# Loading one block's rows in two halves, the first in a tile of its own, in a fused graph-attention kernel

## The chip, the cores and the metric

The kernel runs on one core of a Trainium2 chip. The metric is the device time of one execution in microseconds (us); a kernel's time is the median of several runs. Times inside an execution come from one profiled execution and count from the start of its span.

## What is computed

The input x has 128 batches of 64 rows of 768 numbers, with a 64 by 64 adjacency for each batch. The rows are normalised, then two graph-attention layers follow, and x is added at the end:

```python
h = jnp.maximum(_layernorm(x, axis=-1), 0.0)
for l in range(2):
    m_left  = jnp.einsum('bsh,oh->bso', h, W_left[l])
    m_right = jnp.einsum('bsh,oh->bso', h, W_right[l])
    u_left  = jnp.einsum('bih,bjh->bij', h, m_left) / temper
    u_right = jnp.einsum('bih,bjh->bij', h, m_right) / temper
    u = u_left * adj_tri + u_left * diag_mask + u_right * jnp.swapaxes(adj_tri, 1, 2)
    delta_exp_u = jnp.exp(u) * adj
    attention = delta_exp_u / (jnp.sum(delta_exp_u, axis=2, keepdims=True) + 1e-10)
    h_lin = jnp.einsum('bsh,oh->bso', h, W_lin[l]) + b_lin[l]
    ctx = jnp.matmul(attention, h_lin)
    h = jax.nn.relu(_layer_norm(ctx, ln_a[l], ln_b[l]))
return x + h
```

## The kernel before

**Blocks.** The 128 batches are cut into 16 blocks of 8 batches (512 tokens). A block is needed with features on the partitions (tile ht), while x has tokens on them. Each layer is two passes: pass_one makes the projections for the scores, the scores and the softmax; pass_two makes the linear part, the context and the row norm. The change touches pass_one of the first layer (l = 0).

**Products.** pass_one takes two blocks at a time (U = 0 to 7). For each U, project (L511) runs 29 products (PRODUCTS), a scheme that saves multiplications by forming sums of weight blocks and of token blocks first. Each product is done for the left weight and then for the right one, eight matmuls each (L523). The results lie in PSUM banks (X, Y, Z for left; V and right for right), and read (L293) copies or adds them into the tile m: the first use of a part by ScalarE (ACT, L303), every later one by an add on VectorE (DVE, L221). A bank is used again only when it has been read.

**Slots.** The order of all other work is written out by hand. put(slot, f) puts work at a numbered slot; project calls run four times per product, after half of the matmuls of each side and after its read, so slot 4i is in product i and a U has 116 slots (SLOTS). Within a slot, work is issued in the order in which it was put. Each engine then works through its own queue in order. All DMAs of this stage are issued by SyncE (SP), in program order too.

**The first U.** first (L558) has no ready weights. It loads the raw weights, makes the weight sums product by product on DVE and GpSimd (POOL) (weight_ops), in free 128x512 places, and after each product stores the two weights used to DRAM (keep_weight, L194), from where later U stream them (stream, L197; five of them are issued after product 25). It also prepares blocks 0 and 1 straight from x, in eight row groups n: stats, inverse, norm, turn (transposes on TensorE, L633) and settle. Groups 4 to 7 have slots of their own (L673).

**Blocks 2 to 15 of layer one.** Each goes through DRAM. load_rows (L360) loads a block's rows with eight DMAs into two halves of the buffer ROOM, always the same place; each half holds two of the four row tiles xr[q]. transpose_rows (L384) then gives a list: four statistics (mean_var, DVE, L338 and L339), four empty slots, scale (L394 on ACT, L395 and L396 on DVE), four norms (ACT, L399), two empty slots, four transposes on DVE (L415) into another part of ROOM, and a store of four DMAs (L411) into KEPT. load_h (L371) reads the block back as ht. In U = 0 the third block (u = 2) is loaded at slot 3 and its list begins at slot 26, so its last transposes are at 41 to 44 and its store at 51. The fourth (u = 3) is loaded at 52, right after; its statistics are at 62 to 65, scale at 70, norms at 71 to 74, transposes at 77 to 80, the store at 87, the read back at 103 and the load of the fifth block at 112. These lines set it:

```python
727                        slot = max(slot + 15, (92, 103)[n]) if U == 0 and l == 0 else slot + 15
735                        starts = (8, 52) if U else (26, 62)
```

Of the kernel before, what the change touches and what calls it, by code (L numbers as in the profile page):

```python
# [10 lines left out]
F32 = mybir.dt.float32  # L11
# [6 lines left out]
def kernel(  # L18
# [12 lines left out]
    nc = tc.nc  # L31
    B, S, H = x.shape
    L = w_lin.shape[0]
    P = 128
# [5 lines left out]
    Q = 4  # L40
# [24 lines left out]
    def put(slot, *fs):  # L65
        plan.setdefault(slot, []).extend(fs)
# [73 lines left out]
    def room(n, m):  # L140
        return ROOM[:, n * K2 * D:(n + m) * K2 * D]
# [140 lines left out]
    SLOTS = 4 * NP  # L282
# [29 lines left out]
    KEPT = [[dram.tile([P, C, T], F32, name=f"h{l}_{u}") for u in range(NB)] for l in range(L)]  # L312
# [22 lines left out]
    def mean_var(mv, halves):  # L335
        st = stat.tile([P, 2, 6], F32, name="st", bufs=2)
        for n in range(2):
            nc.vector.bn_stats(st[:, n, :], halves[n])  # L338
        nc.vector.bn_aggr(mv, st)  # L339


    XR = {}
# [3 lines left out]
    def new_ht():  # L346
        turns.rotate(-1)
        return big.tile([P, C, T], F32, name=f"ht{turns[-1]}", bufs=1)

    def rows_tile(pool, g):  # L350
        if pool is not None:
            return pool.tile([P, 2, H], F32, name="x", bufs=2)
        return room(3 * g, 3).rearrange("p (a h) -> p a h", a=2)

    def blocks_tile(pool):
        if pool is not None:
            return pool.tile([P, H // 32, Q, 32], F32, name="xb", bufs=1)
        return room(6, 6).rearrange("p (b q j) -> p b q j", q=Q, j=32)

    def load_rows(l, u, pool=None):  # L360

        XR[l, u] = []
        for g in range(2):
            t = rows_tile(pool, g)
            for a in range(4):
                i = 4 * g + a
                src = x[u * NBB + i] if l == 0 else ROWS[u][i]
                nc.sync.dma_start(t[a * 32:(a + 1) * 32], src.rearrange("(k j) h -> j k h", k=2))
            XR[l, u].extend([t[:, 0, :], t[:, 1, :]])

    def load_h(which, l, u):  # L371
        ht = HT[which, l, u] = new_ht()
        nc.sync.dma_start(ht, KEPT[l][u])
# [10 lines left out]
    def transpose_rows(l, u, pool=None):  # L384

        xr, todo = XR[l, u], []
        if l == 0:
            mv = stat.tile([P, Q, 2], F32, name="mv0", bufs=2)
            sd = stat.tile([P, Q], F32, name="sd0", bufs=2)
            rs = stat.tile([P, Q], F32, name="rs0", bufs=2)  # L390
            nb = stat.tile([P, Q], F32, name="nb0", bufs=2)

            def scale():
                nc.scalar.activation(sd, mv[:, :, 1], AF.Sqrt, bias=eps_in)  # L394
                nc.vector.reciprocal(rs, sd)  # L395
                nc.vector.scalar_tensor_tensor(nb, mv[:, :, 0], -1.0, rs, op0=ALU.mult, op1=ALU.mult)  # L396

            def norm(q):
                nc.scalar.activation(xr[q], xr[q], AF.Relu, bias=nb[:, q:q + 1], scale=rs[:, q:q + 1])  # L399

            norms = [lambda q=q: norm(q) for q in range(Q)]
            stats = [lambda q=q: mean_var(mv[:, q, :], [xr[q][:, :HH], xr[q][:, HH:]]) for q in range(Q)]
            for f in stats + none * (4 * (u < 4)) + [scale] + norms:
                todo.extend([f] + none * (u >= 4))
            todo.extend(none * (2 * (u < 4)))
        xb = blocks_tile(pool)

        def store():
            to = KEPT[l][u].rearrange("(b i) c t -> i c b t", b=4)
            for a in range(4):  # L410
                nc.sync.dma_start(to[:, :, :, a * P:(a + 1) * P],  # L411
                                  xb[a * 32:(a + 1) * 32].rearrange("i (c b) q j -> i c b (q j)", b=4))

        for q in range(Q):
            todo.append(lambda q=q: nc.vector.transpose(  # L415
                xb[:, :, q, :], xr[q].rearrange("p (b j) -> p b j", j=32)))
            todo.extend(none * (l or u >= 4))
        todo.append(store)
        return todo

# [6 lines left out]
    def pass_one(l, aside):  # L427
        with (tc.tile_pool(name=f"ps_one{l}", bufs=1, space=bass.MemoryType.PSUM) as ps,
# [129 lines left out]
            def first():  # L558
# [40 lines left out]
                p = ps_st.tile([P, 2 * TH], F32, name="V")  # L599
# [10 lines left out]
                def stats(n):  # L610
                    mean_var(mv[:, n, :], [xs[n][:, :HH], xs[n][:, HH:]])
                    nc.scalar.activation(sd[:, n:n + 1], mv[:, n, 1:], AF.Sqrt, bias=eps_in)
# [32 lines left out]
                def weight_ops(i, kind):  # L645
                    eng = nc.gpsimd if kind == "r" and i > 1 and i not in (12, 13) else nc.vector
                    return [lambda op=op: weight_op(ss, kind, op, eng) for op in W_OPS if op[0] == i]
# [22 lines left out]
                for i in range(2, NP):  # L670
                    fs = weight_ops(i, "l") + weight_ops(i, "r")
                    put_all(max(2, 4 * (i - 1) - 3), fs)
                for n, (s0, s1, s2, s3) in {4: (3, 4, 5, 8), 5: (6, 7, 8, 12), 6: (13, 14, 15, 19),  # L673
                                            7: (17, 18, 20, 24)}.items():
                    put(s0, lambda n=n: stats(n))
                    put(s1, lambda n=n: inverse(n))
                    put(s2, lambda n=n: norm(n))
                    put(s3, lambda n=n: turn(n), lambda n=n: settle(n))
                put(3, lambda: load_rows(0, 2))
                count = {}  # L680
                for op in X_OPS:
                    n = count[op[0]] = count.get(op[0], 0) + 1
# [28 lines left out]
            for U in range(NU):  # L711
                if U:
                    weights, done = streamed(U)
                if l or U:
                    put_token_ops(l, U, "after")
                if l == 0 and U == 1:
                    for n in range(2):
                        put(20 + 6 * n, lambda n=n: nc.sync.dma_start(KEPT[0][n], HT[1, 0, n]))
                if U + 1 < NU:
                    def block(n, slot):  # L720
                        u = 2 * U + 2 + n
                        *todo, store = transpose_rows(l, u)
                        slot = put_all(slot, todo)
                        put(slot + 6, store)
                        if u + 1 < NB:
                            put(SLOTS - 4 if U == 0 and l == 0 and n else slot + 7, lambda: load_rows(l, u + 1))
                        slot = max(slot + 15, (92, 103)[n]) if U == 0 and l == 0 else slot + 15
                        put(slot, lambda: load_h(1, l, u))
                        if l:
                            put_all(slot + 20, affine(1, l, u))  # L730

                    if l:
                        starts = (6 if U else 20, 48)
                    else:
                        starts = (8, 52) if U else (26, 62)
                    for n, slot in enumerate(starts):
                        put(slot - 1, lambda n=n, slot=slot: block(n, slot))
                    if U:
                        for n in range(2):
                            steps = softmax(2 * U - 2 + n)  # L740
                            slot = put_all(20 + 40 * n if l else (34, 76)[n], steps[:6], 2)
                            slot = put_all(slot, steps[6:] + [lambda n=n: load_adj(2 * U + n)])
                            put(slot + 11, masked(2 * U + n))
                    else:
                        for n in range(2):
                            put((40 if l else 106) + 2 * n, masked(n))
                    put_token_ops(l, U + 1, "before")
                else:
                    for n in range(2):
                        put(12 + 28 * n, lambda n=n: load_h(2, l, n))  # L750
                        put_all(38 + 28 * n, affine(2, l, n))
                    for n in range(2):
                        steps = softmax(2 * U - 2 + n)
                        put_all(put_all(14 + 28 * n, steps[:6], 2), steps[6:])
                    put(40, lambda: load_adj(2 * U))
                    put(54, masked(2 * U))
                    put(SLOTS - 24, lambda: load_adj(2 * U + 1))
                    put(SLOTS - 10, masked(2 * U + 1))
                    put_sums_t((2, l, 0), 94, 2, 85)
                if U in aside:  # L760
                    aside[U]()
                project(U, weights, done)
                assert not plan, sorted(plan)
# [420 lines left out]
```

## Time and profile before

| what | us |
|---|---|
| median of 3 runs | 2721.56 |
| lowest and highest run | 2718.0, 2725.38 |
| the profiled execution | 2719.48 |
| its span | 2717.7 |
| DVE transposes of rows into ROOM in the first 145 us (L415), median of one | 0.97 |
| DMA from 37.39 to 60.34 us, GB/s | 172 |
| DMA from 97.33 to 129.58 us, GB/s | 279 |

In the timelines below, a line is a run of like instructions: its start, its duration, the engine, the line of the code, the operation, the tile written and the tiles read, the shape, the count, and in brackets the idle time ahead of it with what ended that. PE is TensorE. In the slices, a digit is the busy share in tenths of one fortieth of the span (68 us). U = 0 lasts until about 128 us, so it lies in the first two slices. An engine's idle time costs something only if the engine that sets the end waits for it.

### The profile page before, as it was taken

Reading aid. Unit: us, or ns where it says so; the run is one execution under the profiler, and the core shown is the slowest. Engines: PE = TensorE matmul, PEld = TensorE weight load, DVE = VectorE, ACT = ScalarE, POOL = GpSimd, SP = SyncE. Lnnn points to the kernel's source line nnn. Section 1 sums busy time; section 2 is a strip of 40 time slices with the busy share of each in tenths; the row PEclk is TensorE's granted clock in tenths of the full one; section 3 lists DMA queues with packets and bytes.
Section 4 is the critical chain, followed back from the end, with each engine's and each line's share of the span. In section 5 each row is a group of like instructions: output and inputs, shape, how many; then the busy total and the mean of one; then the engine's idle time right before and its main releaser. Section 6 shows DMA issues by size and latency. Waiting matters only on the chain.

```text
span 2717.7 us, 47304 instructions
## 1 busy us (share of the span) xinstructions
PE 2681.2 (99%) x18514; PEld 2302.4 (85%) x18514; DVE 1503.8 (55%) x2458; ACT 829.7 (31%) x1615; POOL 1381.4 (51%) x1071
## 2 busy tenths in 40 slices
PE   8899999999999999999999999999999999999998
PEld 7788888888888888888788888888888888888886
DVE  7655755646556433334334645545446475666667
ACT  4031231321310154454631221221212214444443
POOL 5624244333345766566343235334243286887886
PEclk9999999999999999999999999999999999999999
DMA  7886867869666345557585966858659524655655
GB/s 246 264 288 220 277 203 235 264 202 287 213 204 213 98 136 160 195 155 244 185 280 173 308 201 227 267 194 292 214 195 306 196 97 128 182 159 160 183 158 148
DMA packets 310222, 567.81 MB, mean 209 GB/s; under 512 B 62832, under 2 KB 190064, under 8 KB 301808
## 3 DMA queue, kind: packets, MB, share of 16 engines
q1 hardware_dynamic: 309840, 564.39, 65.0%
q8 instruction: 148, 2.42, 0.4%
q14 instruction: 74, 0.61, 0.1%
q10 hardware_dynamic: 160, 0.39, 0.0%
HBM read 429.40 MB, written 135.27 MB: 208 GB/s over the span
## 4 chain that ended last, share of the span: by engine, by line
PE 93%; DVE 2%; DMA 1%; SPq 1%; issue 0%; ACT 0%; DVEq 0%
PE right L523 17%; PE X L1044 12%; PE X L523 11%; PE V L523 10%; PE Z L523 9%; PE Y L523 9%; PE V L1044 8%; PE Y L1044 6%; PE both L465 5%; PE Z L1044 4%; PE aux L852 2%; PE aux L875 1%; PE Y L875 0%; DMA wp<-ws 0%; DVE m L221 0%
## 5 line engine op out<-in xcount | busy, mean ns | idle before, releaser
L221 POOL TENSOR_TENSOR ts<-ht 128x512 f32<-128x512 f32 x352 | 480.1, 1370 | 158.4 <-PE X L1044 65.8
L221 POOL TENSOR_TENSOR ts<-ht,ts 128x512 f32<-128x512 f32 x192 | 252.8, 1323 | 348.9 <-PE V L523 208.4
L523 PE MATMUL right<-ts,wp 128*128 128x252 f32 (+1 forms) x1632 | 380.9, 376 | 1.5 <-DVE wp L221 1.5
L523 PEld LDWEIGHTS right<-ts,wp 128*128 128x128 f32 x1632 | 310.0, 190 | 40.4 <-DVE wp L221 1.9
L474 POOL TENSOR_TENSOR wm<-adj,tri 128x256 f32<-128x256 f32 x60 | 42.3, 728 | 497.7 <-DMA adj<-in_adj_dram 263.7
L221 DVE TENSOR_TENSOR m<-m,X 128x512 f32<-128x512 f32 x160 | 105.5, 684 | 262.1 <-ACT m L303 183.7
L221 DVE TENSOR_TENSOR m<-m,right 128x504 f32<-128x504 f32 (+1 forms) x304 | 199.4, 673 | 86.3 <-PE right L523 72.4
L1044 PE MATMUL X<-room,ts 128*128 128x256 f32 x1024 | 244.0, 380 | 0.1
L523 PE MATMUL Z<-ts,wp 128*128 128x256 f32 x992 | 234.6, 379 | 0.1
L221 POOL TENSOR_TENSOR ts<-ht,ht 128x512 f32<-128x512 f32 x128 | 163.7, 1289 | 139.3 <-PE right L523 93.6
L1044 PEld LDWEIGHTS X<-room,ts 128*128 128x128 f32 x1024 | 191.7, 190 | 31.7 <-issue 1.8
L523 PEld LDWEIGHTS Z<-ts,wp 128*128 128x128 f32 x992 | 188.3, 190 | 25.2 <-issue 0.4
L523 PE MATMUL X<-ts,wp 128*128 128x256 f32 x872 | 207.5, 381 | 0.0
L523 PE MATMUL V<-ts,wp 128*128 128x252 f32 (+1 forms) x864 | 201.6, 376 | 0.0
L303 ACT ACTIVATE m<-right 128x504 f32<-128x504 f32 (+1 forms) x64 | 36.1, 590 | 509.3 <-PE both L465 489.3
L523 PEld LDWEIGHTS X<-ts,wp 128*128 128x128 f32 x872 | 164.4, 190 | 23.6 <-issue 0.4
L380 ACT ACTIVATE ht<-ht,b_col,a_col 128x512 f32<-128x512 f32 x192 | 140.8, 803 | 142.0 <-DMA ht<-h 142.0
L1044 PE MATMUL Y<-room,ts 128*128 128x256 f32 x768 | 182.5, 379 | 0.0
L523 PEld LDWEIGHTS V<-ts,wp 128*128 128x128 f32 x864 | 164.2, 190 | 20.4
L1044 PEld LDWEIGHTS Y<-room,ts 128*128 128x128 f32 x768 | 145.8, 190 | 20.4 <-issue 0.6
L221 DVE TENSOR_TENSOR m<-m,Y 128x512 f32<-128x512 f32 x144 | 95.8, 683 | 118.4 <-PE Y L523 102.6
L1010 POOL TENSOR_TENSOR z<-z,b 128x768 f32<-128x768 f32 x62 | 112.7, 1831 | 89.7 <-DVE z L1007 89.7
(222 smaller groups left out, 4850.1 us busy)
## 6 DMA issues: line engine op xcount, KB each, us to landing
wp<-ws SPq DMA_DIRECT2D x435, 512.0 KB, 6.2
ht<-h SPq DMA_DIRECT2D x62, 1536.0 KB, 8.7
h<-room SPq DMA_DIRECT2D x112, 384.0 KB, 7.1
z<-z SPq DMA_DIRECT2D x128, 192.0 KB, 3.1
ws<-wp SPq DMA_DIRECT2D x93, 256.0 KB, 4.2
xr<-in_x_dram SPq DMA_DIRECT2D x120, 192.0 KB, 3.7
out_dram<-xr SPq DMA_DIRECT2D x120, 192.0 KB, 2.6
room<-in_x_dram SPq DMA_DIRECT2D x112, 192.0 KB, 5.3
```

Of the source, the lines that this page charges most:

```text
L221: (eng.tensor_add if sign == "+" else eng.tensor_sub)(o, a, b)
L303: nc.scalar.activation(to(o), p, AF.Copy, scale=1.0 if sign == "+" else -1.0)
L380: nc.scalar.activation(ht, ht, AF.Relu, bias=cols[1][:, c:c + 1], scale=cols[0][:, c:c + 1])
L465: nc.tensor.matmul(p[h * S + e:h * S + e + 32, q, e:e + 95], ht[:, c, b * S + e:b * S + e + 32], mb[:, e:e + 95], start=(c == 0), stop=(c ...
L474: nc.gpsimd.tensor_tensor(wm[:, :, k], adj[:, :, 1 - k], tri[:, k].unsqueeze(1).to_broadcast([P, Q, S]), op=ALU.mult)
L523: nc.tensor.matmul(p[:, g], wk[:, c, g * P:(g + 1) * P], tk[:, c, :].rearrange("p (b s) -> p b s", s=S)[:, :, :ns], start=(new and g == c ...
L852: nc.tensor.matmul(cx[k][i, m, :HH], at[j, q, :], hl[j, q, m * HH:(m + 1) * HH], start=True, stop=True)
L875: nc.tensor.matmul(parts[r, k][n][i], at[j, q, :], hl[j, q, cut], start=True, stop=True)
L1010: nc.gpsimd.tensor_add(zs[k], zs[k], rows["b"])
L1044: nc.tensor.matmul(p[:, n], b[t][:, c, r * P:(r + 1) * P], w[s][:, c, :], start=(i in FIRST and i not in PRELOAD and n == c == 0), stop=(c ...
```

## The change

The fourth block's rows (u = 3 of layer one) are loaded in two halves. The first half (four DMAs) gets a tile of its own, "own", of 128 x 2 x 768 numbers, and is loaded at slot 12; the second half is loaded into ROOM at slot 52, where all eight loads were. Statistics of the first half are at slots 57 and 60 and of the second at 66 and 68, scale at 72, norms at 74 to 77, transposes at 79, 81, 82 and 83. The store stays at 87 and the load of the fifth block at 112; the read back goes from 103 to 101. Row group 7 of the first two blocks moves from slots 17, 18, 20, 24 to 15, 16, 18, 23. The transposes and the store move into a function, turned, that transpose_rows calls; for other blocks the order stays what it was.

```diff
-    def load_rows(l, u, pool=None):
+    def load_rows(l, u, pool=None, halves=(0, 1), own=None):
 
-        XR[l, u] = []
-        for g in range(2):
-            t = rows_tile(pool, g)
+        XR.setdefault((l, u), [])
+        for g in halves:
+            t = rows_tile(pool, g) if own is None else own
             for a in range(4):
...
+        def turned(xr, pool):
+            xb = blocks_tile(pool)
+
+            def store():
+                to = KEPT[l][u].rearrange("(b i) c t -> i c b t", b=4)
+                for a in range(4):
+                    nc.sync.dma_start(to[:, :, :, a * P:(a + 1) * P],
+                                      xb[a * 32:(a + 1) * 32].rearrange("i (c b) q j -> i c b (q j)", b=4))
+
+            return [lambda q=q: nc.vector.transpose(
+                xb[:, :, q, :], xr[q].rearrange("p (b j) -> p b j", j=32)) for q in range(Q)], store
...
+            if u == 3:
+                return stats, scale, norms, turned(xr, pool)
...
-                                            7: (17, 18, 20, 24)}.items():
+                                            7: (15, 16, 18, 23)}.items():
...
                 put(3, lambda: load_rows(0, 2))
+                own = sp.tile([P, 2, H], F32, name="own", bufs=1)
+                put(12, lambda: load_rows(0, 3, halves=(0,), own=own))
...
+                        if (l, u) == (0, 3):
+                            stats, scale, norms, (moved, store) = transpose_rows(l, u)
+                            for fs, at in ((stats[:2], (57, 60)), (stats[2:], (66, 68)), ([scale], (72,)),
+                                           (norms, (74, 75, 76, 77)), (moved, (79, 81, 82, 83))):
+                                for f, s in zip(fs, at):
+                                    put(s, f)
+                            put(87, store)
+                            put(SLOTS - 4, lambda: load_rows(l, 4))
+                            put(101, lambda: load_h(1, l, u))
+                            return
...
-                            put(SLOTS - 4 if U == 0 and l == 0 and n else slot + 7, lambda: load_rows(l, u + 1))
-                        slot = max(slot + 15, (92, 103)[n]) if U == 0 and l == 0 else slot + 15
+                            put(slot + 7, lambda: load_rows(l, u + 1, halves=(1,) if (l, u) == (0, 2) else (0, 1)))
+                        slot = max(slot + 15, 92) if U == 0 and l == 0 else slot + 15
...
-                        starts = (8, 52) if U else (26, 62)
+                        starts = (8, 52) if U else (26, 56)
```

More of the change, by code (lines that the diff above doesn't have):

```diff
@@ L405, in transpose_rows @@
             todo.extend(none * (2 * (u < 4)))
[L406 to L416, printed above, removed]
+        moved, store = turned(xr, pool)
+        for f in moved:
+            todo.append(f)
             todo.extend(none * (l or u >= 4))
```

## The prediction

> **What bounds the kernel now.** I read first the busy shares and the 40 slices of the page, to see whether one engine sets the time.
>
> ```profile
> PE 2681.2 (99%) x18514; PEld 2302.4 (85%) x18514; DVE 1503.8 (55%) x2458; ACT 829.7 (31%) x1615; POOL 1381.4 (51%) x1071
> PE   8899999999999999999999999999999999999998
> ```
>
> TensorE is busy for 2681.2 of 2717.7 us, so at most 36.5 us of idle can be won in the whole run, and only the first two slices and the last are below nine. The change touches the first pair of blocks alone (U = 0 of layer one), so second I read TensorE's timeline over the first 145 us. The number in brackets is the idle time ahead of a group and what ended it.
>
> ```profile
> 37.39 0.87 PE L633 MATMUL both<-ident,room 128*128 128x128 f32 x6 [0.95 <-ACT room L620]
> ...
> 48.10 1.97 PE L523 MATMUL Y<-ht,ht 128*128 128x256 f32 x8 [0.42 <-DVE ht L221]
> ...
> 60.34 1.97 PE L523 MATMUL Y<-ts,room 128*128 128x256 f32 x8 [1.72 <-DVE room L221]
> 63.77 1.97 PE L523 MATMUL right<-ts,wp 128*128 128x252 f32 x8 [1.46 <-DVE wp L221]
> ...
> 83.12 1.94 PE L523 MATMUL right<-ht,wp 128*128 128x252 f32 x8 [1.64 <-DVE m L221]
> 87.28 1.97 PE L523 MATMUL Z<-ts,ht 128*128 128x256 f32 x8 [2.22 <-DVE ht L221]
> ...
> 97.33 1.97 PE L523 MATMUL Y<-ts,ht 128*128 128x256 f32 x8 [2.13 <-DVE ht L186]
> ...
> 129.58 1.96 PE L523 MATMUL Y<-ht,wp 128*128 128x256 f32 x8 [1.17 <-DMA wp<-ws]
> ```
>
> Nearly every stop waits for VectorE (DVE). A product without stops takes 3.43 us (69.31 to 72.74), four slots of 0.86 us. Product 17 starts at 79.59 and product 20 at 97.33: 17.74 us where three products need 10.29, so 7.45 us are lost there, restarts included. Third, why DVE is late: its own timeline, then SyncE's (SP).
>
> ```profile
> 75.34 0.83 DVE L221 TENSOR_TENSOR wp<-ht,ht 128x512 f32<-128x512 f32 x1
> 81.16 1.02 DVE L338 BATCH_NORM_STATS2 st<-room 128x6 f32<-128x384 f32 x2 [5.00 <-DMA room<-in_x_dram]
> ...
> 95.88 1.30 DVE L186 TENSOR_SCALAR ht<-wp 128x512 f32<-128x512 f32 x1
> ```
>
> ```profile
> 64.66 4.67 SPq L411 DMA_DIRECT2D h<-room  x4
> 69.38 1.90 SPq L194 DMA_DIRECT2D ws<-room  x1
> 71.33 1.72 SPq L194 DMA_DIRECT2D ws<-wp  x1
> 73.15 4.91 SPq L368 DMA_DIRECT2D room<-in_x_dram  x8
> ```
>
> The fourth block's rows go into the same place (room) as the third's, so their eight loads stand on SP behind the third block's transposes (over at 64.61), its four stores and two weight stores. DVE comes to the first statistics at 76.17, stands 5.00 us until 81.16, and then works without a gap to 97.18 (the negated weight of product 20, L186). That backlog is what TensorE waits for.
>
> **What the Trainium skill says.** "PSUM — Partial Sum Buffer", section "Engine vs sequencer instructions": the queues of ScalarE, VectorE and GpSimdE are strict FIFO. The trace agrees: the m<-right add, ready since 76.3 when its product ended, runs at 82.34, behind the waiting statistics. "DMA: Bandwidth & Descriptors", section "Anatomy of one DMA — SWDGE": DMA engines do not wait on semaphores; the issuing sequencer does, before dispatch. So on SP too: it stood 12.6 us until 64.61 at the first store (L411 <- DVE room L415). "SBUF — State Buffer", section "Who interferes with whom": a VectorE operation with two SBUF inputs contends with a GpSimd one that reads SBUF, and one of them is blocked. It fits the spread of the 128x512 weight sums on DVE, 0.68 us to 1.79 us, while POOL is busy.
>
> **The change part by part**, in this execution's times.
>
> *1. Row group 7 of the first two blocks, slots 17,18,20,24 to 15,16,18,23.* Its statistics and inverse cost DVE 1.01+0.21+0.16+0.21, about 1.6 us, at 32.64. They move ahead of the m<-X adds at 31.43, in front of which DVE idles 3.08 us. Its rows were issued at 17.6, right behind those of group 6, which had landed by 24.55, so no wait is added. ACT no longer stands 2.53 us for these statistics at 33.93, so m<-V on DVE goes from 35.69 to about 34.2. DVE gains 1.5 us. On TensorE the 0.95 (group 7's turn) and the 0.42 at 48.10 go; the two stops at 60.34 and 63.77 (3.18 us) are DVE's chain and stay, 1.5 us earlier. Call this d = 1.5; bounds 0 and 2.5.
>
> *2. First half's four loads at slot 12.* SP issues them between the weight stores of products 2 and 3, about 32 us. 4 x 192 KB is 0.79 MB; at the 339 GB/s that moved from 26 to 37 us this is 2.3 us more for full queues, and up to 4.4 us of SP (half of the 8.85 us that the third block's eight loads took there). What waits behind: weight stores and the adjacency loads. SP later idles 3.8 us (L194 <- DVE ht L221) and the 12.6 us, which hide it. No DVE or POOL operation waits for a weight store before 85 us. I take 0; bounds 0 and 4.4.
>
> *3. Statistics of the first half at slots 57 and 60, then the second half's four loads.* Two times 1.2 us of DVE fall into its idle 71.92 to 74.73 (2.81 us, for PE Y), and nothing waits for them. The four loads left keep their place on SP; the four that landed first before ended the wait at 81.16, so I take the same landing, 81.1 (minus d).
>
> *4. Statistics of the second half at slots 66 and 68.* DVE now does what stood behind the wait: m<-right (to 77.1), two m<-Z (their product ends at 78.05, so to 79.3), the left weight of product 18 (to 79.9). Then it waits 1.2 us instead of 5.0. Queued behind that new wait: m<-right twice, m<-Y twice, the left weight of product 19. With 1.15 us for each statistics pair, 0.6 for each add: 82.3, 83.5, 84.65, 85.85, and that weight at 86.6. TensorE goes from 79.59 to 86.48 without a stop and loses 0.3 at product 19. Further on DVE: m<-right twice (87.8), inverse and offset (1.15, as at 91.31: 88.95), m<-Z (89.55), then for product 20 a sum of 1.5 and a negation of 1.3 as in the trace: 92.4. TensorE would be at product 20 at 90.3 and starts it at 92.6 against 97.33: 4.7 us won, 2.3 still lost.
>
> *5. Norms at 74 to 77, transposes at 79, 81, 82, 83.* The norms (4 x 1.0 us) run on ACT, which has no other work there (idle 28.6 us ahead of L394). The last transposes follow m<-Y and m<-right of product 20: T1 to 96.3, T2 to 97.2, m<-right to 97.8, T3 to 98.8. Before it was 102.42. Minus d, the store's release is 3.6+1.5 = 5.1 us earlier, a little less than TensorE's 4.7+1.5 = 6.2.
>
> *6. What is late next.* The chain of waits goes on from these transposes through SP's stores, ht<-h (111.86, 8.59 us) and the streamed weights (120.52, 8.93 us) to the first product of U = 1:
>
> ```profile
> 111.86 8.59 DMA ht<-h
> 120.52 8.93 DMA wp<-ws
> 129.58 1.96 PE Y L523 x8
> ```
>
> With the same 27.16 us from the last transpose, U = 1 starts 5.1 us earlier. load_h at 101 instead of 103 is the same place on SP: both lie inside product 25, between the weight stores of 24 and 25. From U = 1 on nothing changes and TensorE hardly stops (145 to 250 us: 105.00 busy), so 5.1 us reaches the end.
>
> *Unknown.* TensorE stands 2.90 us at 139.52 in the middle of the scores, released by nothing that the profile shows. I leave it; it may go (-2.9) or another such stop appear (+2.9).
>
> **Sum.** The profiled execution took 2719.48 us (span 2717.7 and 1.8 around it); minus 5.1 that is 2714.4. The median of the runs, 2721.56, lies 2.1 above it, so I forecast 2716.5 for the median.
>
> **The rivals.**
> - *The backlog goes altogether* (larger gain). If the second half lands by 79.9, or the two weight sums of product 20 cost 0.7 instead of 1.5, product 20 starts near 90.3, TensorE has won 7.4+1.5, the last transposes end near 95.5, and U = 1 starts 8.4 to 8.9 earlier; with the 2.90 stop gone too, 11.7. Time 2710 to 2713. For it: four loads instead of eight leave SP and the DMA engines 2.4 us. Against it: the stores ahead of these loads are the same.
> - *The transfer decides U = 1 anyway.* DMA is near full from 109 us to 145; if stores, ht<-h and weight stream are bound by bytes, U = 1 starts at 128 to 129.5 whatever VectorE did: 2720.5. Against it: DMA is at 30% or less from 91 to 105 us, so the stores have room to move up.
> - *Slower.* The four loads of step 2 push SP's weight stores back by 4.4 us while DVE has no slack (36 to 71 us), and weight sums that reuse a stored slot wait for them, as POOL does once now (3.0 us <- DMA ws<-wp). One such wait on DVE moves all later steps by 4.4 and leaves 0.7 of the 5.1; two give 2721.6 - 5.1 + 8.8 = 2725.3. It decides from 5.1 us of such waits on. Against it: no such wait on DVE today, and slots are reused oldest first.
>
> **How the numbers follow.** My forecast has 0.48, the larger gain 0.33, the bound transfer 0.11, slower 0.08. What a measurement can tell from no change is 0.3%, 8.2 us: faster is below 2713.4. Of the larger gain 0.28 lies there, and 0.05 of my own case (d at 2.5, the 2.90 gone): faster 0.33. Of the slower case 0.05 lies above 2729.7; the rest is within: 0.62. The likeliest case spans 2712 to 2719; the range for 8 in 10 is 2710 to 2721: it takes in the larger gain and most of the bound transfer.
>
> **What would show it.** In DVE's timeline statistics of own near 71 to 75 us without a wait; a wait of about 1 us at the statistics of room near 80, none of 5; TensorE's stops at 37.39 and 83.12 gone and that at product 20 about 2 us; the last transpose near 97; the first streamed weight near 115, U = 1 near 124.5. I am wrong if DVE waits more than 3 us for the second half, if weight sums wait for ws stores, or if U = 1 doesn't move.

## The result and the profile after

| | before | after |
|---|---|---|
| median of 8 runs, us | 2721.16 | 2712.26 |
| lowest and highest run, us | 2718.0, 2725.38 | 2710.28, 2719.53 |
| the profiled execution's span, us | 2717.7 | 2708.5 |
| start of product 20 of U = 0, us | 97.33 | 88.64 |
| end of the fourth block's last transpose, us | 102.42 | 94.93 |
| start of U = 1, us | 129.58 | 122.30 |

The ratio of after to before is 0.997, 95% interval 0.9958 to 0.9983: faster, by 4.6 to 11.4 us, some 0.3% of the whole. The profiles of the table are one execution each. Later profiles of the same two kernels have U = 1 at 129.30 before and 122.99 after (see the experiments), so at U = 1 the gain is 6.3 to 7.3 us. TensorE's timeline of the changed kernel follows; the columns are start, duration, engine, line, operation, tiles, shape, count, and in brackets the idle time ahead and what ended it.

```profile
35.07 0.82 PE L640 MATMUL both<-ident,room 128*128 128x128 f32 x6
...
57.13 1.97 PE L530 MATMUL Y<-ts,room 128*128 128x256 f32 x8 [0.67 <-DVE room L221]
60.55 1.97 PE L530 MATMUL right<-ts,wp 128*128 128x252 f32 x8 [1.46 <-DVE wp L221]
...
78.11 1.86 PE L530 MATMUL right<-ht,wp 128*128 128x252 f32 x8
79.81 1.89 PE L530 MATMUL Z<-ts,ht 128*128 128x256 f32 x8
...
88.64 1.97 PE L530 MATMUL Y<-ts,ht 128*128 128x256 f32 x8 [1.82 <-DVE ht L186]
...
122.30 1.97 PE L530 MATMUL Y<-ht,wp 128*128 128x256 f32 x8 [2.58 <-DMA wp<-ws]
```

The stops at group 7's turn (0.95), at 48.10 (0.42), at the right side of product 17 (1.64) and at product 18 (2.22) are gone, the one at product 12 has shrunk from 1.72 to 0.67, and the 1.46 right after it is the same. Besides it two stay: 1.82 us at product 20, and the stop at U = 1, which has grown from 1.17 to 2.58. VectorE's and SyncE's timelines show why:

```profile
68.64 1.00 DVE L338 BATCH_NORM_STATS2 st<-own 128x6 f32<-128x384 f32 x2
69.68 0.21 DVE L339 BATCH_NORM_AGGREGATE mv<-st 128x2 f32<-128x12 f32 x1
69.81 0.97 DVE L338 BATCH_NORM_STATS2 st<-own 128x6 f32<-128x384 f32 x2
...
76.08 1.14 DVE L221 TENSOR_TENSOR ht<-wp,ht 128x512 f32<-128x512 f32 x1
77.15 1.00 DVE L338 BATCH_NORM_STATS2 st<-room 128x6 f32<-128x384 f32 x2
...
87.19 1.30 DVE L186 TENSOR_SCALAR ht<-wp 128x512 f32<-128x512 f32 x1
```

```profile
31.18 2.10 SPq L368 DMA_DIRECT2D own<-in_x_dram  x4
...
61.45 4.66 SPq L394 DMA_DIRECT2D h<-room  x4
...
69.95 2.26 SPq L368 DMA_DIRECT2D room<-in_x_dram  x4
...
94.95 4.58 SPq L394 DMA_DIRECT2D h<-room  x4
...
104.56 0.47 SPq L373 DMA_DIRECT2D ht<-h  x1
...
112.93 8.73 SPq L197 DMA_DIRECT2D wp<-ws  x5
```

The first half's statistics run at 68.6 without a wait, and those of the second half follow the weight sum ahead of them with no idle time that the timeline reports: the 5.00 us are gone. DVE still works without a gap from 74.88 to the negation at 87.19, so product 20 still waits for it. The last three SP lines are the chain into U = 1: the store that follows the last transpose, the third block's read back, and the streamed weights, which SP issues only when that read back has landed, 8.4 us after its issue. TensorE comes to U = 1 8.7 us earlier than before, and this chain only 7.3 us earlier; so the stop there grew.

### The profile page after: what moved, and what is told of

Its sections match the earlier page's. It is cut to its first block, busy times and chain, and to the rows that moved or that the text cites. A ratio compares the mean times of both kernels' runs of the same rounds, so it can differ in the third digit from the quotient of the medians.

```text
span 2708.5 us, 47300 instructions
## 1 busy us (share of the span) xinstructions
PE 2677.3 (99%) x18514; PEld 2304.5 (85%) x18514; DVE 1502.9 (55%) x2458; ACT 829.2 (31%) x1615; POOL 1380.6 (51%) x1071
## 4 chain that ended last, share of the span: by engine, by line
PE 94%; DVE 2%; DMA 1%; SPq 1%; issue 0%; ACT 0%; DVEq 0%
PE right L530 17%; PE X L1063 12%; PE X L530 11%; PE V L530 10%; PE Z L530 9%; PE Y L530 9%; PE V L1063 8%; PE Y L1063 6%; PE both L472 5%; PE Z L1063 4%; PE aux L871 2%; PE aux L894 1%; PE Y L894 0%; DMA wp<-ws 0%; PE Z L472 0%
## 5 line engine op out<-in xcount | busy, mean ns | idle before, releaser
L530 PEld LDWEIGHTS Z<-ts,wp 128*128 128x128 f32 x992 | 188.8, 190 | 24.8 <-issue 0.4
```

Source lines behind the costliest of these rows:

```text
L530: nc.tensor.matmul(p[:, g], wk[:, c, g * P:(g + 1) * P], tk[:, c, :].rearrange("p (b s) -> p b s", s=S)[:, :, :ns], start=(new and g == c ...
```

## The experiments

**Before once more**, to see how far one profile's anchors (the starts of product 12, product 20 and U = 1) vary. No edit.

> The kernel before once more, for how far one profile's anchors vary from execution to execution. Expected: product 12 at 60.3, product 20 at 97.3, U = 1 at 129.6, each within 0.5 us; if they vary by 1 us or more, differences of that size between the other profiles say nothing.

Product 12 at 60.35, product 20 at 97.07, U = 1 at 129.30: all within 0.3 us. The landing that ended DVE's wait came at 80.36 instead of 81.16, so a single landing varies by 0.8. The changed kernel's two profiles lie further apart: 57.13 and 57.70, 88.64 and 89.22, 122.30 and 122.99. Differences of less than about 0.7 us between single profiles say little. The one time was 2722.12.

**Group 7's slots alone.**

```diff
 (the kernel before)
-                                            7: (17, 18, 20, 24)}.items():
+                                            7: (15, 16, 18, 23)}.items():
```

> The kernel before with row group 7 at slots 15, 16, 18, 23 and nothing else. If the two parts of the change add up (my theory): product 12 starts near 57.2 us instead of 60.3, DVE still waits about 5 us for the fourth block's rows, product 20 starts near 94.1 and U = 1 near 126.4 instead of 129.6, so some 3.2 us less than before. If the gain of group 7 is only kept because the split removes the later wait (rival): product 12 is early, but U = 1 starts at 129 to 129.6 and the time is that of before.

TensorE's timeline of this run:

```profile
57.64 1.97 PE L523 MATMUL Y<-ts,room 128*128 128x256 f32 x8 [1.18 <-DVE room L221]
...
94.17 1.97 PE L523 MATMUL Y<-ts,ht 128*128 128x256 f32 x8 [0.58 <-DVE ht L186]
...
126.67 1.97 PE L523 MATMUL Y<-ht,wp 128*128 128x256 f32 x8 [1.43 <-DMA wp<-ws]
```

This is as the theory of two parts has it. The wait of 5 us is there (5.21). Product 12 is 2.7 us earlier and U = 1 2.9: this part's gain reaches U = 1 without the split. The median was 2717.64 against 2720.12, ratio 0.9995 [0.9986, 1.0003], so in whole runs this part alone isn't told from no change; only the profile shows it (2.6 us at U = 1 against the second profile of the kernel before).

**The split alone.**

```diff
 (the changed kernel)
-                                            7: (15, 16, 18, 23)}.items():
+                                            7: (17, 18, 20, 24)}.items():
```

> The changed kernel with row group 7 back at 17, 18, 20, 24. Theory of two parts that add: product 12 at 60.3 as before, no wait of 5 us on DVE, product 20 near 91.9 and U = 1 near 125.5, some 4.1 us less than before. Rival (the split alone makes nearly all of it, group 7's stops being filled anyway): U = 1 at 123 or earlier.

Product 12 at 59.44, product 20 at 90.95, U = 1 at 124.97 with a stop of 2.94; 2716.66 against 2720.12, ratio 0.9985 [0.9978, 0.9991]. There is no wait for the rows. Product 12 and product 20 came 0.9 us earlier than expected; the run with four dead loads below shows why. The two parts win 2.9 and 4.6 us at U = 1, together 7.5; the change wins 7.3, or 6.6 by its second profile. They add up as far as single profiles can tell.

**Late statistics without the split.**

```diff
 (the changed kernel)
-                own = sp.tile([P, 2, H], F32, name="own", bufs=1)
-                put(12, lambda: load_rows(0, 3, halves=(0,), own=own))
...
-                            for fs, at in ((stats[:2], (57, 60)), (stats[2:], (66, 68)), ([scale], (72,)),
+                            for fs, at in ((stats, (66, 67, 68, 69)), ([scale], (72,)),
...
-                            put(slot + 7, lambda: load_rows(l, u + 1, halves=(1,) if (l, u) == (0, 2) else (0, 1)))
+                            put(slot + 7, lambda: load_rows(l, u + 1))
```

> The changed kernel without the split: all eight loads into ROOM at slot 52, all four statistics at slots 66 to 69, all other slots as changed. If what counts is only that the statistics no longer stand ahead of the PSUM adds of products 15 and 16 (rival): product 20 near 88.6 and U = 1 near 122.5 as with the change. If the 2.4 us of DVE work that the split moves ahead of the landing count too (my sum, step 3): product 20 between 91 and 92.5 and U = 1 between 124.5 and 126.

DVE waits 1.01 us for the rows and then has four statistics among the adds and weight sums:

```profile
78.73 1.02 DVE L338 BATCH_NORM_STATS2 st<-room 128x6 f32<-128x384 f32 x2 [1.01 <-DMA room<-in_x_dram]
```

TensorE of this run:

```profile
86.30 1.97 PE L530 MATMUL X<-ts,wp 128*128 128x256 f32 x8 [2.39 <-DVE wp L221]
...
93.19 1.97 PE L530 MATMUL Y<-ts,ht 128*128 128x256 f32 x8 [3.23 <-DVE ht L186]
...
126.81 1.97 PE L530 MATMUL Y<-ht,wp 128*128 128x256 f32 x8 [2.54 <-DMA wp<-ws]
```

U = 1 starts 4.5 us later than with the change, and no earlier than with group 7 alone (126.67). Product 20 and U = 1 lie 0.7 and 0.8 us past what I expected of my sum, so that sum was short too. Putting all statistics later only moves the stops from products 17 and 18 to 19 and 20. A rival is that the split wins because four loads land sooner than eight (7.0 us after the first issue with the change, 8.2 here). The last transpose ends at 99.47 here and at 94.93 with the change, 4.5 us apart. Of these, 0.5 is there at product 12 already (57.64 and 57.13), 1.1 more at the first statistics of room (78.73 and 77.15), which is the landing, and 3.0 comes after them, where two more statistics of 1.15 us each stand. So most of what the split wins is the DVE work done ahead of the landing, and the earlier landing is the smaller part. The one time was 2718.49.

**Four dead loads at slot 12**, for the cost of the early loads on SP.

```diff
 (the kernel before)
                 put(3, lambda: load_rows(0, 2))
+                own = sp.tile([P, 2, H], F32, name="own", bufs=1)
+
+                def dead_loads():
+                    for a in range(4):
+                        src = x[3 * NBB + a].rearrange("(k j) h -> j k h", k=2)
+                        nc.sync.dma_start(own[a * 32:(a + 1) * 32], src)
+
+                put(12, dead_loads)
```

> The kernel before with four more loads of 192 KB at slot 12 into a tile that nothing reads (the fourth block is still loaded whole at slot 52). Step 2 of the prediction, cost 0: product 12 at 60.3 and U = 1 at 129.6, both within 0.4 us. Rival (SP's weight stores are late and weight sums wait for them): product 12 or U = 1 later by 2.3 to 4.4 us, with DVE waiting for ws stores before 64 us.

Product 12 at 59.57 and U = 1 at 128.72: neither within 0.4 nor later, but 0.8 and 0.6 to 0.9 earlier than in the two profiles of the kernel before. The rival of the prediction, that SP's late weight stores hold up VectorE, is refuted: DVE waits for none. (The one time was 2719.16.) Where the small gain comes from stands in the DVE timelines, first of the kernel before, then of this run:

```profile
40.68 1.79 DVE L221 TENSOR_TENSOR wp<-ht,wp 128x512 f32<-128x512 f32 x1
```

```profile
40.59 0.99 DVE L221 TENSOR_TENSOR wp<-ht,wp 128x512 f32<-128x512 f32 x1
```

and in POOL's timeline of this run:

```profile
39.77 1.27 POOL L221 TENSOR_TENSOR ht<-wp,ht 128x512 f32<-128x512 f32 x1 [0.57 <-DMA ws<-ht]
```

In the kernel before POOL has the operation of that last line at 39.25, for 1.45 us. That was all but over when DVE's sum began, and DVE's sum fell in with POOL's next one, from 40.67 to 41.93. Here POOL comes to it half a microsecond later, after a weight store, and is done with it at 41.04. Both times DVE's sum ends 0.54 us after the sum of POOL that was under way when it began, so here it takes 0.8 us less. The last section has this for all profiles.

**The third block's read back ahead of the store.** This and the next are aimed at the two stops that are left.

```diff
 (the changed kernel)
-                        slot = max(slot + 15, 92) if U == 0 and l == 0 else slot + 15
+                        slot = max(slot + 15, 85) if U == 0 and l == 0 else slot + 15
```

> The changed kernel with the third block's read back (load_h) at slot 85, ahead of the fourth block's store, instead of 92. My reading of the chain: the first streamed weight waits for this 1.5 MB read only because SP issued it eight DMAs earlier, behind the store; so it is issued near 92, the first streamed weight near 109.5 instead of 112.9, and U = 1 starts near 119.8 with its stop of 2.6 us gone. Rival (bytes decide): the stream still lands near 122 and U = 1 starts there.

SyncE's timeline of this run, then TensorE's at U = 1:

```profile
90.10 0.32 SPq L373 DMA_DIRECT2D ht<-h  x1
94.33 4.83 SPq L394 DMA_DIRECT2D h<-room  x4
106.81 0.57 SPq L373 DMA_DIRECT2D ht<-h  x1
108.45 8.86 SPq L197 DMA_DIRECT2D wp<-ws  x5
```

```profile
118.93 1.89 PE L530 MATMUL Y<-ht,wp 128*128 128x256 f32 x8
```

The first streamed weight is issued at 108.45 instead of 112.93, and U = 1 starts at 118.93 with no stop. Bytes do not decide: with the same transfers in another order the stream is issued 4.5 us sooner and U = 1 starts 3.4 us sooner. The one time was 2709.83.

**The weight sums of product 20 three slots earlier.**

```diff
 (the changed kernel)
-                    put_all(max(2, 4 * (i - 1) - 3), fs)
+                    put_all(70 if i == 20 else max(2, 4 * (i - 1) - 3), fs)
```

> The changed kernel with the weight sums of product 20 at slots 70 to 73 instead of 73 to 76. The stop of 1.8 us at product 20 goes. Since DVE works without a gap from 77 us to the last transpose, that transpose stays near 94.9 and U = 1 near 122.2, with the stop there grown to 4.4 (my theory: the last transpose decides). Rival (TensorE's own lateness decides): U = 1 at 120.5.

The stop at product 20 goes, the last transpose ends at 94.29, and U = 1 starts at 121.65 with a stop of 3.91:

```profile
121.65 3.55 PE L530 MATMUL Y<-ht,wp 128*128 128x256 f32 x8 [3.91 <-DMA wp<-ws]
```

Product 20 starts 1.9 us earlier than with the change (86.74), the last transpose and U = 1 0.6 us earlier, which is no more than the two profiles of the changed kernel differ by. TensorE was early and gave it back: the last transpose decides. The one time was 2714.13.

**Both edits**, measured twice, the second time alongside the changed kernel.

> Both edits on the changed kernel. If the two readings hold: no stop at product 20, U = 1 near 118.7 to 119.2, some 3.3 us less than the changed kernel and 11 to 12 less than before (ratio 0.9957). If bytes decide: U = 1 near 122 and the time of the changed kernel.

> The changed kernel once more, on the same chip as the next run, for a direct comparison. Expected: 2711 to 2713, ratio to before near 0.997; U = 1 near 122.3; in the profile no or one stretch of 3.4 us at half clock before 150 us.

> Both edits on the changed kernel once more: 2708 to 2710, ratio to before near 0.9957, 3 us below the changed kernel of the same call; U = 1 near 118.7.

| | median | before, alongside | ratio | interval | U = 1 |
|---|---|---|---|---|---|
| both edits | 2708.81 | 2719.47 | 0.9958 | 0.9945 to 0.9972 | 118.67 |
| changed kernel again | 2712.45 | 2719.95 | 0.9977 | 0.9970 to 0.9983 | 122.99 |
| both edits again | 2709.04 | 2719.95 | 0.9966 | 0.9952 to 0.9979 | 118.12 |

Side by side, both edits have the lower median by 3.4 us, near the 3.3 expected, and three of their five runs lie below all 21 of the changed kernel (2709.39 and up). The intervals against the kernel before overlap, so in whole runs the step from the changed kernel is likely rather than proved. In the two pairs of profiles U = 1 is 3.6 and 4.9 us earlier. Since the read back alone already brings 118.93, the earlier sums add little.

**Fewer warm-up transposes**, for the unknown stop in the scores.

```diff
 (the changed kernel)
-                for _ in range(34):
+                for _ in range(26):
```

> The changed kernel with 26 instead of 34 warm-up transposes on TensorE at the very start. This is about the stop of 2.6 to 4.1 us in the middle of the first scores of U = 1, which stands after 154 of 192 matmuls in every profile so far. If it hangs on the place in TensorE's instruction stream, it moves by the eight matmuls, to after 162. If it hangs on the scores themselves (their data or a release), it stays after 154. Otherwise as the changed kernel: U = 1 near 122.3.

TensorE's timeline of the changed kernel, then of this run:

```profile
125.89 3.45 PE L472 MATMUL both<-m,ht 128*32 128x95 f32 x154
132.09 1.02 PE L472 MATMUL both<-m,ht 128*32 128x95 f32 x38 [2.75 <-issue]
```

```profile
128.94 3.62 PE L472 MATMUL both<-m,ht 128*32 128x95 f32 x162
135.90 1.49 PE L472 MATMUL both<-m,ht 128*32 128x95 f32 x30 [3.34 <-issue]
```

Eight transposes fewer ahead, and the stop stands eight matmuls later; in the twelve other profiles, whatever the order of the other work, it stands after 154. It hangs on the place in TensorE's instruction stream, not on the scores. What happens at that place the profile does not show. In this run U = 1 started at 123.66 instead of the expected 122.3, because the streamed weights were released 9.5 us after the read back was issued instead of 8.4. The one time was 2719.05.

## Why the prediction was right, and which terms were off

The forecast of 2716.5 had the right direction and mechanism; the measured 2712.26 lies 4.2 us below it, and the second median, 2712.45, 4.1 below. The gain was 8.9 us the first time and 7.5 the second, where the prediction had put 0.62 on a difference within 8.2 us and 0.33 on a larger gain. Against the sum, 5.1 us, the first pair of profiles shows 7.28 at U = 1 and 9.2 at the end, the second pair 6.31 and 5.6.

The 4.1 us by which the first pair passes the sum are made up of 0.3 from the start of the kernel, 1.4 from step 1, 0.7 from steps 4 and 5, 0.2 less from the chain of step 6, and 1.9 after U = 1. The first and most of the last are chance, as shown below; the terms that the prediction mis-sized are those of steps 1 and 4. No large error hid another.

- **Step 1, group 7's slots.** d was sized at 1.5, bounds 0 and 2.5. Product 12 moved by 3.21. Of that 0.34 was there already at the right side of product 3 (25.80 instead of 26.14), ahead of what the step touches. It is chance: the second profile of the changed kernel has 26.18 there. So 2.9 belongs to the change; group 7 alone gives 2.4 in the same count, the split alone 0.9 and the dead loads 0.7, so the early loads have a share in it. The m<-V add, which I put 1.5 earlier, came 2.24 earlier, 1.9 without the 0.34. The rest I left out: the six DVE instructions from m<-Y up to the third block's first statistics took 5.52 us before (36.88 to 42.40), and 4.35 with group 7 alone, 4.72 with the dead loads, 4.88 with the change. The work is the same; a weight sum of 1.79 became 1.28 and a negation of 1.38 became 0.72, while another sum went from 0.69 to 1.20. This is the skill's contention with POOL that the prediction itself named, and then priced at nothing. The last section has its size.
- **Step 2, the four early loads.** Cost 0 was right in that nothing waits to a loss; the dead loads even moved product 12 by 0.8 us the good way, by when POOL came to its sums.
- **Step 3, first half's statistics.** As forecast: they run in DVE's idle time before m<-Y, which shrank from 2.81 to 0.51.
- **Step 4, second half.** Mis-sized, to the safe side: 1.2 us of wait were put in, and none came. The forecast had the rows land at 81.1 less d, that is 79.6; they landed at 76.93. The four loads were issued 3.2 us earlier than the eight had been, not 1.5, and their landing was shorter. The landing was taken over from the eight loads (8.0 us from the first issue to the statistics). With four loads it was 7.0, by the chain of waits of the changed kernel:

```profile
69.95 0.40 SPq L368
...
71.78 5.15 DMA room<-in_x_dram
76.92 0.03 issue
76.95 0.05 DVEq L338
```

Eight loads took 7.2 to 8.2 us in the profiles in which DVE waited for them, so four rather than eight may not be the whole reason; that is open. Not all of the 1.2 was won: the left weights of products 18 and 19 took DVE 1.1 us each, where I had put in 0.6 and 0.75. Product 17 to product 20 took 12.26 us, forecast 13.0, before 17.74; the stop left at product 20 was 1.82, forecast 2.3.
- **Steps 5 and 6, the chain into U = 1.** Right in kind, and the strongest part: from the end of the last transpose to U = 1 it is 27.16 and 27.14 us in the two profiles before, 27.37 and 27.49 in those after, 27.40 with group 7 alone, 27.74 with the split alone, 27.34 without the split, 27.05 with the dead loads and 27.36 with the early sums (28.54 with fewer warm-ups). It breaks only where the read back moves: 24.3 and 24.8 with both edits, and no more than 24.6 with the read back alone, where TensorE did not wait for it. The transposes came 7.5 earlier instead of 5.1, through the start, d and step 4, and U = 1 7.3. TensorE, itself 8.7 us early at product 20, gave 1.4 of it back at the stop at U = 1.
- **The unknown stop.** 2.90 before, 2.75 after (4.12 and 3.09 in the second profiles): left alone was right.
- **From U = 1 on "nothing changes".** Not quite. Between the first and the third product of U = 1 the lead grows from 7.28 to 9.07 us, of which 0.15 is the unknown stop. The windows view shows the rest: length, then for each engine busy us and count, then TensorE's granted clock, DMA's share and GB/s. First the kernel before, then the changed one:

```profile
140.00:145.00 5.00, 5.00 (x39) 4.03 (x29) 2.05 (x5) 1.08 (x2) 3.48 (x3) 0.66 1.04 281
```

```profile
133.00:136.50 3.50, 3.50 (x21) 3.10 (x17) 1.21 (x4) 1.08 (x2) 3.21 (x3) 1.00 1.05 244
136.50:140.00 3.50, 3.50 (x18) 2.91 (x16) 3.16 (x9) 0.60 (x1) 0.00 (x0) 1.00 0.72 278
```

Right after its stop in the scores the kernel before runs at a clock of 0.66 for 5 us, a loss of 1.7; the changed kernel keeps 1.00 at the same place. The sum had no term for it. It is luck of this pair: the second profile of the changed kernel loses 5.1 us to half clock up to 160 us, that of the kernel before 3.4 (last section), and there the lead shrinks after U = 1.

Of the rivals, the larger gain had U = 1 8.4 to 8.9 us earlier (0.33 of the chance). The measured 7.28 and 6.31 lie between it and the forecast. One of its conditions came true, the landing before 79.9, but DVE's backlog did not go altogether, since product 20 still waits 1.82. That the median gained 8.9 us too is a coincidence: in the profiles 1.7 us of the lead at the end is clock. The bound transfer is refuted by the change itself and by the early read back, and the slower case by the dead loads.

## What to carry to other kernels

A load that must wait for its buffer, in front of statistics in a strict queue, is paid by everything queued behind them; giving half of it a tile of its own pays because the work on that half can be done before the landing, not because the rest is done later. After such a gain ask which chain is released next: here it ran from the last transpose through one queue of DMAs, its length stayed within 27.0 to 27.8 us in nine of the ten profiles that kept its order, and moving one 1.5 MB read ahead of a store took about 3 us off it. Work that is only made early on an engine off that chain (the sums of product 20) is given back.

## What the hardware showed unexpectedly

- **A stop of TensorE can cost a second time.** The Trainium skill, "TensorE: Matmul & The Clock Gate", Part 1, says that the clock is halved after an idle window of about 3.4 us. In the 13 profiles, up to 160 us, the granted clock fell to 0.50 seventeen times, for 3.4 us thirteen times and for 6.8 us four times: 1.7 or 3.4 us lost. Each time it began between 0.9 us before and 1.4 us after the end of a stop of 2.21 us or more. So the length of the half clock agrees with the skill's window, but here the stop can be shorter than the window, and the measurement decides: 14 of the 17 stops were below 3.4 us. It is not the same in each execution: 25 stops were that long, eight of them cost nothing more, and no stop of 2.13 us or less was followed by half clock. The changed kernel's first profile has none, though two of its stops, 2.58 and 2.75, are long enough; its second has three stretches of 3.4 us. The stop that the change left at U = 1 is of this kind, the 1.17 us before it was not.
- **Single runs scatter with the clock.** The 21 runs of the changed kernel's second time: where the mean clock was 0.999 they took 2709.4 to 2711.9 us, at 0.998 2710.8 to 2713.5, at 0.997 2715.0 to 2716.5, and the one at 0.996 2719.6. Differences of 3 us between single runs are therefore no evidence for or against an edit; the anchors in the profile are better.
- **A sum on VectorE waits for a sum on POOL.** The DVE sum ahead of the third block's first statistics took 1.79, 1.29, 0.99 and 0.72 us in four kernels. In the 13 profiles, from 30 to 110 us, 84 of DVE's 128x512 sums of two SBUF operands (those that the timeline shows singly) began while POOL was in a sum: 83 of them ended 0.54 to 0.56 us after POOL's. The 78 with nothing on POOL took 0.65 to 0.69 us, and so did the eight that began while POOL was in a negation. DVE's adds of one SBUF and one PSUM operand took 0.62 to 0.69 us whatever POOL did, 218 of them beside it. So moving work by half a microsecond changed the length of other work by as much. It is the contention that the prediction cites from the skill, with its price here; only POOL's negations, which read SBUF too, held up no sum.
- **TensorE stopped for 2.6 to 4.1 us at one place of its instruction stream in every profile**, and the place followed the count of instructions ahead of it. The cause stays open.
